# A Mamba-2 block with a LoRA branch on one core: the group norm's root and reciprocal on four rows, spread through DRAM, and the convolution one step later

## The chip, the core and the metric

The kernel runs on one core of a Trainium2 chip, in fp32 throughout. The metric is the device time of one execution in microseconds (us). The core has a matrix engine (PE in the profile, with its weight loads shown apart as PEld), a vector engine (DVE), a scalar engine (ACT), a general engine (POOL) and SyncE (SP), which here only issues DMAs. Each engine takes its own instructions in a fixed order, and semaphores hold an instruction until what it needs is there.

## What is computed

For 2048 tokens of width 1024, with `xn = layernorm(x)`:

```python
proj = xn @ in_proj_w.T                    # gate 4096 | x 4096, B 1024, C 1024 | dt 64
xBC  = silu(depthwise_conv4(proj[4096:10240]) + bias)
state_t = state_{t-1} * exp(dt*A) + (dt*x_t) B_t        # 64 heads of 64, 8 groups
y_t  = C_t . state_t + D * x_t
var  = mean(y_g * y_g) over the 512 channels of each of 8 groups
yn   = y_g * rsqrt(var + 1e-5) * norm_weight * silu(gate)
out  = x + yn @ out_proj_w.T + (xn @ W_base.T + b_base + top-2 of 8 LoRA experts of rank 16)
```

The change touches the line `yn = ...`: how the root and the reciprocal are made, one number for each token and group.

## The kernel before

The channels lie on the 128 partitions and the tokens along the free dimension. All big products are done by a seven-product Strassen-Winograd scheme; one product of the scheme is eight `MATMUL` records (four steps of the contraction, each two records in fp32).

The work falls into three stretches. A start (to about 180 us) normalizes the first 1024 tokens and makes the first products. The long middle (to about 2685 us) does two things at once: a *stream* of in-projection products (`stream`, `pair`, lines 450 to 495), and the scan. The last stretch is the out-projection.

The scan goes over 32 *blocks*: two halves of the sequence s, eight groups g, two halves of 512 tokens. A block has four *slots* c = 0 to 3 of 128 tokens. The loop at lines 983 to 1078 writes the order of a slot by hand: one product of the stream; `scan_b` of this slot (the products `ps_y`, `ps_e`, `ps_st` and the additions on DVE after them); the first third of `scan_a` of the next slot (the decay scan L688); a second product; the second third (`ps_cb`, the copies L698, L700, L705 on ACT, the product L709 on DVE); two more products; the last third (the transposes `ps_xt`, the scalings `xdt` L720 and `xdd` L728 on ACT); and one more product in some slots. Side work is dealt out among these products in a list `parts`, one entry for each. The PE instructions, the Silu activations and the scalings L720 and L728 keep this program order. For the others it is only a priority: the framework's planner orders each engine's instructions before the run, and may put one ahead of its place if it expects it to be ready. Nothing is reordered while the kernel runs.

A product's result waits in one of four PSUM buffers until DVE or ACT takes it. The seventh product of a scheme adds into the buffer that the fifth one left: DVE must have added that one out (`ev`, L531) within the one product that lies between.

The side work that matters here, for block b:

- Slot 0: `norm_mean` of the block before (L810): one matmul with a matrix of ones sums 512 channels of squares onto all 128 partitions (`ps_nv`), and ACT takes the root to `rms` (128x512, L815). Then `norm_gate` (L818), one step to each of the products 1, 2 and 3 and the last ones after them: the reciprocal on 128x512 (L821), four multiplications by the norm's weight and `rms` (L824), two by the gate (L832), each followed by the store of two channel tiles to DRAM (`y<-xg`, L833).
- Slots 1 and 2: `conv` of the next block (L629), seven steps, called four and four times (the eighth finds nothing left). A step is three DVE operations (L646) on one channel tile; steps 1 and 2 are for B and C (`bc`), steps 3 to 6 for x (`xg`). Step 3 also issues the first tap of all four x tiles on ACT (L640). The tile `xg` has two buffers, so the next block's convolution writes where the block before had its y: it waits until both stores `y<-xg` have landed.
- Slot 3: the squares of this block (L804, L806, L807).
- Blocks 2, 5, 8 and 11 load a piece of the second 1024 tokens into the gate's buffer (`sg`) in slot 1 and normalize it. Blocks 3, 6, 9 and 12, in slot 0, turn that piece's small projection into dt and decays: a chain of some 25 short DVE operations (L311 to L329, the polynomial L323 among them), whose exponential `ex` (L330) ACT must make.

Besides the four buffers of the stream, PSUM has four banks with one buffer each, called `y`, `e`, `st` and `aux`. Before the change `aux` serves `ps_cb`, `ps_xt` and `ps_nv`; `st` serves `ps_st`, the layer norm's sums, `ps_tot` and `ps_sm`.

Of the kernel before, what the change touches and what calls it, by code (L numbers as in the profile page):

```python
# [8 lines left out]
F32 = mybir.dt.float32  # L9
AF = mybir.ActivationFunctionType  # L10
# [5 lines left out]
H = 64  # L16
# [11 lines left out]
P = 128  # L28
TS = 1024
NS = L // TS  # L30
TB = 512
Q = 128
NQ = TB // Q
# [5 lines left out]
NSM = H + NE + NE * RANK  # L39
# [3 lines left out]
def mamba_lora_kernel(  # L43
# [17 lines left out]
    nc = tc.nc  # L61
# [16 lines left out]
    def mm(*args, **kw):  # L78
        tc.keep_in_program_order(nc.tensor.matmul(*args, **kw))  # L79
# [11 lines left out]
    ones = const.tile([P, P], F32, name="ones")  # L91
    nc.vector.memset(ones, 1.0)
    ident = const.tile([P, P], F32, name="ident")
    make_identity(nc, ident)
    eps = const.tile([P, 1], F32, name="eps")
    nc.vector.memset(eps, EPS)


# [87 lines left out]
    def over_channels(of, bank, name):  # L186
        ps = ps_one.tile([P, 2 * Q], F32, tag=bank, name=f"ps_{name}")
        for k, part in enumerate(of):
            mm(ps, ones, part, start=(k == 0), stop=(k == len(of) - 1))
        return ps  # L190
# [53 lines left out]
    def ln_next(s, i):  # L244

        t = piece_of[s, i]
        flat = t.rearrange("p k n q -> p k (n q)")

        of = halved(flat, f"{s}_{i}", ev, "ev")
        yield  # L250
        ps = over_channels(of, "st", f"mean_{s}_{i}")
        mean = lp.tile([P, 2 * Q], F32, tag="lnmean", name=f"mean_{s}_{i}")
        nc.scalar.activation(mean, ps, AF.Copy, scale=1.0 / DM)
        yield
        sqs = []
        for h in range(2):
            normal(flat[:, 4 * h : 4 * h + 4, :], mean, ALU.subtract)
            for k in (4 * h, 4 * h + 2):
                sq = ev.tile([P, 2, 2 * Q], F32, tag="ev", name=f"lsq_{s}_{i}_{k}")
                nc.scalar.activation(sq, flat[:, k : k + 2, :], AF.Square)  # L260
                sqs.append(sq)
            nc.vector.tensor_tensor(sqs[2 * h], sqs[2 * h], sqs[2 * h + 1], ALU.add)
            if h:
                nc.vector.tensor_tensor(sqs[0], sqs[0], sqs[2], ALU.add)
            yield
        ps = over_channels([sqs[0][:, 0, :], sqs[0][:, 1, :]], "st", f"var_{s}_{i}")
        std = lp.tile([P, 2 * Q], F32, tag="lnstd", name=f"std_{s}_{i}")
        nc.scalar.activation(std, ps, AF.Sqrt, bias=eps, scale=1.0 / DM)
        nc.vector.reciprocal(std, std)
        yield  # L270
        for h in range(2):
            normal(flat[:, 4 * h : 4 * h + 4, :], std, ALU.mult)
            yield
        b11, b12 = t[:, 0:KH, 0, :], t[:, 0:KH, 1, :]
        b21, b22 = t[:, KH:KT, 0, :], t[:, KH:KT, 1, :]
        cols = slice(i * Q, (i + 1) * Q)
        t4, t1, t2, t3 = (
            ev.tile([P, KH, Q], F32, tag="ev", name=f"t_{s}_{i}_{j}") for j in range(4)
        )
        nc.vector.tensor_tensor(t1, b12, b11, ALU.subtract)  # L280
        nc.vector.tensor_tensor(t2, b22, t1, ALU.subtract)
        yield
        nc.vector.tensor_tensor(t4, b21, t2, ALU.subtract)
        nc.vector.tensor_tensor(t3, b22, b12, ALU.subtract)
        for j, src in enumerate((b11, b21, b22, t4, t1, t2, t3)):
            nc.sync.dma_start(xop_d[s][j][:, :, cols], src)
        yield
# [9 lines left out]
    def small(s, i, chunks, sm, home):  # L297
# [32 lines left out]
        nc.scalar.activation(ex, at, AF.Exp)  # L330
        yield

        ps = ps_one.tile([P, nch, H], F32, tag="st", name=f"ps_tot_{n}")
        mm(
            ps.rearrange("p c h -> p (c h)"), ones, at.rearrange("p c h -> p (c h)"),
            start=True, stop=True,
# [268 lines left out]
    def steps(gen, n):  # L605

        return [lambda: next(gen, None) for _ in range(n)]
# [71 lines left out]
    def scan_a(s, g, half, c):  # L679

        key = s, g, half, c
        n = f"{s}_{g}_{half}_{c}"
        dab, ecp = decay_of.pop(key)
        hs = slice(g * HG, (g + 1) * HG)
        cs = slice(c * Q, (c + 1) * Q)

        es = p1.tile([P, HG, Q], F32, tag="es", name=f"es_{n}")
        nc.vector.tensor_tensor_scan(  # L688
            es.rearrange("p h t -> p (h t)"), dab.rearrange("p h t -> p (h t)"), here, 0.0,
            ALU.mult, ALU.add,  # L690
        )
        yield
        xg, bc = xbc_of[s, g, half]
        psm = ps_one.tile([P, 2, Q], F32, tag="aux", name=f"ps_cb_{n}")
        mm(psm[:, 0, :], bc[:, 0, cs], bc[:, 1, cs], start=True, stop=True)
        transpose(psm[:, 1, :], bc[:, 0, cs])
        cbm = p2.tile([P, Q], F32, tag="cbm", name=f"cbm_{n}")
        nc.scalar.copy(cbm, psm[:, 0, :])  # L698
        bt = p2.tile([P, Q], F32, tag="bt", name=f"bt_{n}")
        nc.scalar.copy(bt, psm[:, 1, :])  # L700

        psy = ps_one.tile([P, 4, Q], F32, tag="y", name=f"ps_y_{n}")
        for j in range(4):
            at = 4 * g + j
            nc.scalar.activation(  # L705
                psy[:, j, :], xg[:, j, cs], AF.Copy, scale=dsk[:, at : at + 1]
            )
        ms = dab
        nc.vector.tensor_tensor(  # L709
            ms, es, cbm.unsqueeze(1).to_broadcast([P, HG, Q]), ALU.mult  # L710
        )
        yield
        pst = ps_one.tile([P, 4, Q], F32, tag="aux", name=f"ps_xt_{n}")
        for j in range(4):
            transpose(pst[:, j, :], xg[:, j, cs])
        xdt = p2.tile([P, HG, HP], F32, tag="xdt", name=f"xdt_{n}")
        x_t = pst.rearrange("p j (a q) -> p (j a) q", q=HP)
        for h in range(HG):
            at = g * HG + h
            ins = nc.scalar.activation(  # L720
                xdt[:, h, :], x_t[:, h, :], AF.Copy,
                scale=dt_of[s][:, half * NQ + c, at : at + 1],
            )
            tc.keep_in_program_order(ins)

        xdd = p1.tile([P, HG, HP], F32, tag="xdd", name=f"xdd_{n}")
        for h in range(HG):
            ins = nc.scalar.activation(  # L728
                xdd[:, h, :], xdt[:, h, :], AF.Copy, scale=es[:, h, Q - 1 : Q]
            )  # L730
            tc.keep_in_program_order(ins)
        mid_of[key] = ms, ecp, bt, xdt, xdd, psy
        yield
# [74 lines left out]
        yield  # L808

    def norm_mean(s, g, half):  # L810
        y = y_of[s, g, half]
        ps = ps_one.tile([P, TB], F32, tag="aux", name=f"ps_nv_{s}_{g}_{half}")
        mm(ps, ones, y[:, 0, :], start=True, stop=True)
        std = p1.tile([P, TB], F32, tag="rms", name=f"rms_{s}_{g}_{half}")
        nc.scalar.activation(std, ps, AF.Sqrt, bias=eps, scale=1.0 / (4 * P))  # L815
        norm_of[s, g, half] = std

    def norm_gate(s, g, half):  # L818

        xg, std = xbc_of[s, g, half][0], norm_of[s, g, half]  # L820
        nc.vector.reciprocal(std, std)  # L821
        yield
        for j in range(4):
            nc.vector.scalar_tensor_tensor(  # L824
                xg[:, j, :], xg[:, j, :], nw[:, 4 * g + j : 4 * g + j + 1], std,
                ALU.mult, ALU.mult,
            )
        yield
        at = s * TS + half * TB
        for j in (0, 2):  # L830
            two = xg[:, j : j + 2, :]
            nc.vector.tensor_tensor(two, two, sg_of[s, g, half][:, j : j + 2, :], ALU.mult)  # L832
            nc.sync.dma_start(y_d[g][:, j : j + 2, at : at + TB], two)  # L833
            yield
# [148 lines left out]
    for b, blk in enumerate(blocks):  # L983
# [16 lines left out]
        for c in range(NQ):  # L1000
# [16 lines left out]
            if c in (1, 2) and nxt:  # L1017
                if c == 1:
                    conv_steps = conv(*nxt)
                side += steps(conv_steps, 4)  # L1020
            if c == 2 and after != 0:
                side += [lambda: load_gate(*blk)]
            if b == 1 and c < 2:
# [17 lines left out]
                load_decays(*second)  # L1041
            next(a, None)
            if c == 0 and prev:
                out = norm_gate(*prev)
                parts[1:4] = [[*p, lambda: next(out, None)] for p in parts[1:4]]
                parts[3] += [lambda: next(out, None)] * 2
            if c == NQ - 1:
                sq = norm_squares(*blk)
                parts[1] += steps(sq, 2)
# [18 lines left out]
                next(ln)  # L1068
            if after == 0 and c == 3:
                sm = lp.tile([P, 2, NSM], F32, tag="sm", name=f"sm_{piece[0]}_{piece[1]}")  # L1070
                ps = ps_one.tile([P, 2, NSM], F32, tag="st", name=f"ps_sm_{piece[1]}")
                for h in range(2):
                    small_mm(ps[:, h, :], lambda k: piece_of[piece][:, k, h, :])
                nc.scalar.copy(sm, ps)
                rest = small(*piece, slice(piece[1], 2 * NQ, NQ), sm, home)
                load_gate(*blk)
            if (after, c) in ((1, 1), (2, 0)):
                next(rest)
    norm_mean(*blocks[-1])
    for _ in norm_gate(*blocks[-1]):  # L1080
        pass
    wo_ctx.close()
# [325 lines left out]
```

## Time and profile before

| | |
|---|---|
| median of 3 runs | 3439.4 us (3437.9 to 3439.51) |
| the profiled execution | 3437.5 us, of which span 3435.7 us (1.8 us around it) |
| PE busy | 3404.6 us, 99% of the span |
| DVE busy | 2410.5 us, 70% |
| ACT busy | 1338.9 us, 39% |
| POOL busy | 697.2 us, 20% |
| reciprocal of the norm, L821 | 32 of 3345 ns |
| root of the norm, L815 | 32 of 687 ns |
| sum of the norm, `ps_nv` | 64 records (two for each block), 33.0 us busy |
| clock granted to PE | 0.998 of full speed |

The profile is one execution. Busy time is the time in which an engine has at least one instruction under way; for PE the ends of the matmuls are modelled, so an interval between two starts is often the better measure. A wait is idle time of an engine just ahead of an instruction, put down to whatever released it last. A number in square brackets in a timeline row is such a wait.

### The profile page before, as it was taken

How to read it: one execution, taken by the hardware profiler on the slowest of the kernel's cores; microseconds unless marked ns; L12 is line 12 of the kernel's file. 1: busy time of each engine (PE TensorE's matmuls, PEld its weight loads, DVE VectorE, ACT ScalarE, POOL GpSimd, SP SyncE). 2: the span in 40 equal slices, each digit the busy share in tenths (PEclk: the TensorE clock that was granted, in tenths of full speed). 3: DMA queues.
4: the chain of work that ended last, by engine and by line, in shares of the span. 5: the costliest groups of instructions: out<-in, count | busy, mean ns of one | idle time of the engine just before them, and what ended most of it. 6: DMA issues, size and time to landing. Idle time of an engine off the chain costs nothing.

```text
span 3435.7 us, 38674 instructions
## 1 busy us (share of the span) xinstructions
PE 3404.6 (99%) x12820; PEld 1989.8 (58%) x12820; DVE 2410.5 (70%) x2733; ACT 1338.9 (39%) x3694; POOL 697.2 (20%) x443
## 2 busy tenths in 40 slices
PE   9999999999999999999999999999999999999999
PEld 7444544544545544544455454454454588888888
DVE  7547776877877867777777877777875466566665
ACT  2245454554555454545545455555453000000000
POOL 4123223222222211332222332222321000000000
PEclk9999999999999999999999999999999999999999
DMA  6546655655666676887778787877777777585654
GB/s 236 190 166 198 209 184 187 216 183 196 207 196 209 196 261 219 287 261 242 235 246 256 235 255 249 254 237 240 242 237 260 256 274 242 195 300 187 214 164 144
DMA packets 530327, 769.85 MB, mean 224 GB/s; under 512 B 35152, under 2 KB 264656, under 8 KB 527440
## 3 DMA queue, kind: packets, MB, share of 16 engines
q1 hardware_dynamic: 530128, 767.39, 68.7%
q8 instruction: 102, 1.67, 0.2%
q14 instruction: 97, 0.79, 0.1%
HBM read 516.64 MB, written 250.61 MB: 223 GB/s over the span
## 4 chain that ended last, share of the span: by engine, by line
PE 87%; DVE 8%; issue 2%; DMA 2%; ACT 2%; SPq 0%; DVEq 0%; ACTq 0%
PE ps_x_x L79 12%; PE ps_x_w L79 8%; PE ps_a_x L79 8%; PE ps_y_x L79 8%; PE ps_x_g L79 8%; PE ps_y_w L79 6%; PE ps_a_w L79 6%; PE ps_y_g L79 5%; PE ps_a_g L79 5%; PE ps_y L79 3%; PE ps_e L79 3%; PE ps_st L79 3%; PE ps_x_b L79 2%; DVE xg L646 2%; PE ps_a_b L79 2%
## 5 line engine op out<-in xcount | busy, mean ns | idle before, releaser
L83 POOL TENSOR_TENSOR state<-state,tot 128x512 f32<-128x512 f32 x112 | 150.2, 1341 | 1307.6 <-PE ps_e L79 1175.7
L688 DVE TENSOR_TENSOR_SCAN es<-dab,here 128x1024 f32<-128x1024 f32 x128 | 303.5, 2371 | 82.6 <-ACT xdd L728 81.3
L646 DVE SCALAR_TENSOR_TENSOR xg<-rawx,cw,xg 128x512 f32<-128x512 f32 x384 | 338.3, 929 | 16.8 <-ACT xg L640 15.9
L79 PE MATMUL ps_x_w<-t,w 128*128 128x256 f32 x1344 | 303.8, 379 | 0.0
L720 ACT ACTIVATE xdt<-ps_xt,dt 128x64 f32<-128x64 f32 x1024 | 223.0, 331 | 203.6 <-PE ps_xt L88 203.6
L79 PEld LDWEIGHTS ps_x_w<-t,w 128*128 128x128 f32 x1344 | 255.4, 190 | 41.5 <-issue 7.7
L705 ACT ACTIVATE ps_y<-xg,dsk 128x128 f32<-128x128 f32 x512 | 190.2, 371 | 222.5 <-DVE xg L770 192.9
L1345 ACT COPY s<-ps_a_w 128x512 f32<-128x512 f32 x28 | 16.4, 585 | 636.2 <-PE ps_a_w L79 555.6
L728 ACT ACTIVATE xdd<-xdt,es 128x64 f32<-128x64 f32 x1024 | 261.7, 387 | 0.0
L83 POOL TENSOR_TENSOR wo<-wo 128x512 f32<-128x512 f32 (+1 forms) x112 | 211.9, 1892 | 6.8
L709 DVE TENSOR_TENSOR dab<-es,cbm 128x1024 f32<-128x1024 f32 x128 | 177.6, 1388 | 39.3 <-ACT cbm L698 39.0
L79 PE MATMUL ps_a_w<-q,w 128*128 128x256 f32 x896 | 202.5, 379 | 0.0
L79 PEld LDWEIGHTS ps_a_w<-q,w 128*128 128x128 f32 x896 | 170.2, 190 | 23.6 <-issue 0.5
L79 PE MATMUL ps_x_x<-op_again,s_x 128*128 128x512 f32 x384 | 172.7, 592 | 0.0
L79 PE MATMUL ps_y_x<-op_again,s_x 128*128 128x512 f32 x384 | 172.7, 592 | 0.0
L79 PE MATMUL ps_a_x<-op_again,a_x 128*128 128x512 f32 x384 | 172.7, 592 | 0.0
L79 PEld LDWEIGHTS ps_y<-dab,xdt 128*64 128x64 f32 x2048 | 112.8, 137 | 102.9 <-issue 40.8
L79 PE MATMUL ps_x_x<-op,s_x 128*128 128x512 f32 x368 | 165.5, 592 | 0.0
L79 PE MATMUL ps_y_x<-op,s_x 128*128 128x512 f32 x368 | 165.5, 592 | 0.0
L79 PE MATMUL ps_a_x<-op,a_x 128*128 128x512 f32 x368 | 165.4, 592 | 0.0
L646 DVE SCALAR_TENSOR_TENSOR bc<-rawb,cw,bc 128x512 f32<-128x512 f32 x192 | 163.8, 885 | 1.9 <-ACT bc L640 1.3
L531 DVE TENSOR_TENSOR ev<-ps_x_x,s_x 128x512 f32<-128x512 f32 x94 | 64.4, 686 | 129.3 <-PE ps_x_x L79 124.2
(238 smaller groups left out, 6152.1 us busy)
## 6 DMA issues: line engine op xcount, KB each, us to landing
w<-w SPq DMA_DIRECT2D x196, 512.0 KB, 3.7
dab<-da_d SPq DMA_DIRECT2D x128, 512.0 KB, 5.4
raw<-ev SPq DMA_DIRECT2D x192, 256.0 KB, 3.3
a_x<-in_w_in_dram SPq DMA_DIRECT2D x168, 256.0 KB, 4.0
w<-wo SPq DMA_DIRECT2D x96, 448.0 KB, 4.3
ecp<-run_d SPq DMA_DIRECT2D x256, 128.0 KB, 4.0
gate<-ev SPq DMA_DIRECT2D x128, 256.0 KB, 3.6
sg<-gate SPq DMA_DIRECT2D x32, 1024.0 KB, 7.8
```

Source lines behind the costliest of these rows:

```text
L79: tc.keep_in_program_order(nc.tensor.matmul(*args, **kw))
L83: ins = nc.gpsimd.tensor_tensor(*args)
L531: nc.vector.tensor_tensor(e, ps, add, alu)
L646: nc.vector.scalar_tensor_tensor(dst[:, i, :], raw[:, i, k : k + TB], cw[:, ti, k : k + 1], dst[:, i, :], ALU.mult, ALU.add,)
L688: nc.vector.tensor_tensor_scan(es.rearrange("p h t -> p (h t)"), dab.rearrange("p h t -> p (h t)"), here, 0.0, ALU.mult, ALU.add,)
L705: nc.scalar.activation(psy[:, j, :], xg[:, j, cs], AF.Copy, scale=dsk[:, at : at + 1])
L709: nc.vector.tensor_tensor(ms, es, cbm.unsqueeze(1).to_broadcast([P, HG, Q]), ALU.mult)
L720: ins = nc.scalar.activation(xdt[:, h, :], x_t[:, h, :], AF.Copy, scale=dt_of[s][:, half * NQ + c, at : at + 1],)
L728: ins = nc.scalar.activation(xdd[:, h, :], xdt[:, h, :], AF.Copy, scale=es[:, h, Q - 1 : Q])
L1345: nc.scalar.copy(s1, pa)
```

## The change

The norm's sum is made with four matmuls instead of one. Matmul c has as its weights four columns of which only column c is ones, and 128 tokens as its moving operand; together they leave a tile of 4 rows of 128 tokens. Root and reciprocal are made on this 4x128 tile. A new function `norm_spread` makes the reciprocal, stores the tile to DRAM (2 KB) and loads it back to all 128 partitions (256 KB written). It is called in slot 0; `norm_gate` moves to slot 1, all three steps ahead of the convolution's there. The convolution makes three steps in slot 1 and four in slot 2. The transposes `ps_xt` move to the bank `st`; the layer norm's sums, `ps_tot` and `ps_sm` move from `st` to `aux`.

```diff
-    eps = const.tile([P, 1], F32, name="eps")
+    row_of = const.tile([P, 8], F32, name="row_of")
+    nc.vector.memset(row_of, 0.0)
+    nc.vector.memset(row_of[:, NQ - 1 : NQ], 1.0)
+    eps = row_of[:, 7:8]
     nc.vector.memset(eps, EPS)
...
-        ps = over_channels(of, "st", f"mean_{s}_{i}")
+        ps = over_channels(of, "aux", f"mean_{s}_{i}")
...
-        ps = over_channels([sqs[0][:, 0, :], sqs[0][:, 1, :]], "st", f"var_{s}_{i}")
+        ps = over_channels([sqs[0][:, 0, :], sqs[0][:, 1, :]], "aux", f"var_{s}_{i}")
...
-        ps = ps_one.tile([P, nch, H], F32, tag="st", name=f"ps_tot_{n}")
+        ps = ps_one.tile([P, nch, H], F32, tag="aux", name=f"ps_tot_{n}")
...
-        pst = ps_one.tile([P, 4, Q], F32, tag="aux", name=f"ps_xt_{n}")
+        pst = ps_one.tile([P, 4, Q], F32, tag="st", name=f"ps_xt_{n}")
...
     def norm_mean(s, g, half):
         y = y_of[s, g, half]
-        ps = ps_one.tile([P, TB], F32, tag="aux", name=f"ps_nv_{s}_{g}_{half}")
-        mm(ps, ones, y[:, 0, :], start=True, stop=True)
-        std = p1.tile([P, TB], F32, tag="rms", name=f"rms_{s}_{g}_{half}")
-        nc.scalar.activation(std, ps, AF.Sqrt, bias=eps, scale=1.0 / (4 * P))
-        norm_of[s, g, half] = std
+        n = f"{s}_{g}_{half}"
+        ps = ps_one.tile([NQ, Q], F32, tag="aux", name=f"ps_nv_{n}")
+        for c in range(NQ):
+            mm(
+                ps, row_of[:, NQ - 1 - c : 2 * NQ - 1 - c], y[:, 0, c * Q : (c + 1) * Q],
+                start=(c == 0), stop=(c == NQ - 1),
+            )
+        rms = p1.tile([P, TB], F32, tag="rms", name=f"rms_{n}")
+        nc.scalar.activation(
+            rms[0:NQ, 0:Q], ps, AF.Sqrt, bias=eps[0:NQ], scale=1.0 / (4 * P)
+        )
+        norm_of[s, g, half] = rms
+
+    def norm_spread(s, g, half):
+        rms = norm_of[s, g, half]
+        std = rms[0:NQ, 0:Q]
+        n = f"{s}_{g}_{half}"
+        nc.vector.reciprocal(std, std)
+        std_d = dram.tile([NQ, Q], F32, tag=f"std_d_{n}", name=f"std_d_{n}")
+        nc.sync.dma_start(std_d, std)
+        nc.sync.dma_start(
+            rms, std_d.rearrange("c t -> (c t)").unsqueeze(0).to_broadcast([P, TB])
+        )
...
-        xg, std = xbc_of[s, g, half][0], norm_of[s, g, half]
-        nc.vector.reciprocal(std, std)
-        yield
+        xg, rms = xbc_of[s, g, half][0], norm_of[s, g, half]
         for j in range(4):
             nc.vector.scalar_tensor_tensor(
-                xg[:, j, :], xg[:, j, :], nw[:, 4 * g + j : 4 * g + j + 1], std,
+                xg[:, j, :], xg[:, j, :], nw[:, 4 * g + j : 4 * g + j + 1], rms,
                 ALU.mult, ALU.mult,
             )
...
-                side += steps(conv_steps, 4)
+                side += steps(conv_steps, 3 if c == 1 else 4)
...
             if c == 0 and prev:
+                parts[1].insert(0, lambda: norm_spread(*prev))
+            if c == 1 and prev:
                 out = norm_gate(*prev)
-                parts[1:4] = [[*p, lambda: next(out, None)] for p in parts[1:4]]
-                parts[3] += [lambda: next(out, None)] * 2
+                parts[1][:0] = steps(out, 3)
...
-                ps = ps_one.tile([P, 2, NSM], F32, tag="st", name=f"ps_sm_{piece[1]}")
+                ps = ps_one.tile([P, 2, NSM], F32, tag="aux", name=f"ps_sm_{piece[1]}")
...
     norm_mean(*blocks[-1])
+    norm_spread(*blocks[-1])
     for _ in norm_gate(*blocks[-1]):
         pass
```

## The prediction, made before the changed kernel was built or run

> **What bounds the kernel now.** I read the engines' busy time first, for the engine at its limit.
>
> ```profile
> PE 3404.6 (99%) x12820; PEld 1989.8 (58%) x12820; DVE 2410.5 (70%) x2733; ACT 1338.9 (39%) x3694; POOL 697.2 (20%) x443
> ```
>
> PE is busy in all but 31 us of the span. A change that unloads DVE and ACT can gain only what PE now waits for them. So the second view is PE's waits between 180 and 2690 us, the scan (in all, times, longest):
>
> ```profile
> PE ps_y L79 <- ACT xdt L720: 6.9, 5, 4.6
> PE ps_x_x L79 <- DVE ev L531: 3.6, 3, 1.3
> PE ps_x_g L79 <- DVE ev L531: 3.3, 6, 1.1
> PE ps_e L79 <- ACT da L346: 1.7, 2, 0.9
> PE ps_st L79 <- ACT xdd L728: 1.4, 4, 0.4
> PE ps_mean L79 <- DVE half L183: 1.0, 1, 1.0
> PE ps_nv L79 <- ACT xdt L720: 0.6, 1, 0.6
> ```
>
> Some 19 us, and no DMA among them. Third, the timeline at the longest of these waits (block 3, end of slot 0), from the answers for DVE, ACT and PE:
>
> ```profile
> 431.08 3.35 DVE L821 RECIPROCAL rms<-rms 128x512 f32<-128x512 f32 x1
> ...
> 442.44 1.21 DVE L832 TENSOR_TENSOR xg<-xg,sg 128x1024 f32<-128x1024 f32 x1
> ...
> 448.30 0.28 DVE L329 TENSOR_TENSOR at<-dt,na 128x128 f32<-128x128 f32 x1
> ...
> 449.02 0.31 ACT L330 ACTIVATE ex<-at 128x128 f32<-128x128 f32 x1
> 449.24 1.73 ACT L720 ACTIVATE xdt<-ps_xt,dt 128x64 f32<-128x64 f32 x8
> ...
> 449.59 0.69 PE L79 MATMUL ps_y<-dab,xdt 128*64 128x128 f32 x3 [4.57 <-ACT xdt L720]
> ```
>
> The releaser is ACT, but ACT was idle: it stood at the exponential L330, which waited for the polynomial on DVE, and DVE had the reciprocal and the norm's multiplications in the same slot (busy 24.70 of the 26 us from 424 on). The later waits for `xdt` at the end of slot 0 (blocks 6, 9 and 12: 0.7, 0.4 and 0.7 us) have the same order of rows. The waits for `ev` lie elsewhere: five of nine in slot 1 of the later half. Fourth, block 24 by slots (from a slot's first `ps_y` to the next):
>
> ```profile
> 2084.60:2105.50 20.90, 20.90 (x74) 10.36 (x73) 17.73 (x17) 8.61 (x27) 1.04 (x1) 1.00 0.68 216
> 2105.50:2124.50 19.00, 17.77 (x68) 8.90 (x67) 15.89 (x19) 10.93 (x29) 7.18 (x5) 1.00 0.68 206
> 2124.50:2142.00 17.50, 17.50 (x68) 8.87 (x67) 7.64 (x8) 6.64 (x24) 5.70 (x3) 1.00 0.88 299
> 2142.00:2161.40 19.40, 18.64 (x70) 9.07 (x69) 15.59 (x16) 10.68 (x30) 5.65 (x3) 1.00 0.76 221
> ```
>
> The fourth figure after the window is DVE's busy time: 17.7, 15.9, 7.6, 15.6 us. Slot 2 stands half empty. The chain there runs reciprocal, norm multiplications, `y<-xg` (2099.19, 5.03 us), the next block's convolution until 2119, `ev` at 2120.12, and PE waits 1.23 us.
>
> **Part by part.** The rows for the prices:
>
> ```profile
> L821 DVE RECIPROCAL rms<-rms 128x512 f32<-128x512 f32 x32 | 107.0, 3345 | 0.9 <-ACT rms L815 0.9
> L318 DVE RECIPROCAL u<-u 128x128 f32<-128x128 f32 x4 | 3.8, 952 | 0.0
> L79 PE MATMUL ps_e<-bc,state 128*128 128x128 f32 x960 | 139.9, 289 | 1.7 <-ACT da L346 1.7
> L79 PE MATMUL ps_nv<-sq,ones 128*128 128x512 f32 x64 | 33.0, 597 | 0.7 <-ACT xdt L720 0.6
> ```
>
> *Reciprocal.* Three quarters of the elements in a row go: 3.345 - 0.952 = 2.39 us a block, 77 us of DVE in all, none of it on PE's path except at the waits above. The root falls from 0.687 us to about that of the 128x128 exponential (0.31): 12 us of ACT, beside PE's work.
>
> *The moved multiplications.* Four of 0.74 and two of 1.2 us, 5.4 us a block, leave their place in slot 0. With the reciprocal that is 7.8 us less DVE before the polynomial's end in blocks 3, 6, 9 and 12. The exponential was late by 4.6 us at most. Gain: 4.6+0.7+0.4+0.7 = 6.4, the `ps_st` waits that follow three of them, 3 x 0.36 = 1.1, and the slow records after the longest. On that last: the Trainium skill ("TensorE: Matmul & The Clock Gate", What's actually happening) says that the clock halves after an idle window of about 3.4 us; after the 4.6 us wait the starts of the next six or so records lie 1.2 us further apart than elsewhere, and after none of the waits under 2 us. Sum 8.7 us. What is late next there: `ev`, 2.6 us before the exponential, not waited for. Bounds: 0, if the planner moves the multiplications back ahead of the polynomial and they wait for the load, to 8.7. I take 8: DVE has 7.8 us of room for a delay of 4.6.
>
> *Banks.* `ps_nv` no longer waits for `xdt` (0.6), nor the first `ps_xt` for the copy `bt` (0.6): gain 1.2. `ps_xt` now waits for the state's addition L784, which in block 24 ends at 2091.9, 6 us ahead of it: 0. The moved sums wait for the copies of L700, done a product earlier: 0. Without that cover each would cost a copy, 0.3 us.
>
> *Sum on PE.* Two records of 512 columns become eight of 128. Here a rule speaks against the change. The same page (Back-to-back issue gap) gives for sustained matmuls 81 ns at 128 columns and 131 at 512, so quartering a matmul makes it 4 x 81/131 = 2.5 times as long: from the trace's two starts (429 and 522 ns, 0.95 us) to 2.35 us, +1.4 a block, +45 us in all. The trace says otherwise: starts lie 429 ns apart at 512 columns and 112 (median) to 128 (mean) at 128 columns in `ps_e`, whose weights also change with each matmul. By that, eight take 0.90 to 1.02 us: -2 to +2 us in all. The row decides; I take 0. The extreme bound is a weight load of 190 ns unhidden at each, 1.52 us, +18 in all; `ps_e` excludes it.
>
> *Spread.* Two more DMAs a block, 64 in all, on SP. A small store (`s_x_d<-s_x`) lands in 2.1 us, `run_d` in 4.1; loads of the broadcast kind in 4.0 (`ecp`) to 5.4 us (`dab`). So `rms` is there 6 to 9.5 us after the reciprocal, I take 7.5. The skill's "DMA: Bandwidth & Descriptors" (Anatomy of one DMA) has 2.0 us fixed and 436 GB/s, an estimate of 4.6 us for both: by that the multiplications could start in block 24 at 2093.7, as they do now (2093.56); by the rows at 2096 to 2098. SP stands still for the reciprocal and the store's landing, 2 to 4 us a block, and behind it lie weights (L423), stores of results (L535) and decays (L665, L673). It stands still as long already (up to 9.6 us for POOL, 7.0 for DVE), and PE waits for no DMA in the scan, since weights are loaded a pair ahead: 0. Without that cover it would be 31 x 3 = 93 us.
>
> *Norm and convolution later.* From DVE's free time in slot 0 the planner may take the multiplications as soon as it expects `rms`, so y lands 3 us later than now at the least, or a slot (18) at the most. Half of the convolution's 11 us on `xg` falls into slot 2, where DVE is idle 9.9 of 17.5 us. Silu of `xg` ends at 2131.4 in block 24, its readers begin at 2147.8: 16 us of cover, 0. The gate buffer is free later for the pieces, which land at 359.4 and 616.5, 15 us before their first use (375.1, 631.0): 0. Unhidden, they would cost up to 3 us in each of four blocks.
>
> *`ev` waits in slot 1* (1.09, 1.31, 1.23, 0.68, 1.10: 5.4 us): less convolution in the slot, but possibly the multiplications. Bounds: all gone, -5.4; or 1.2 us in each of the 31 slots, +37. I take 0, nearest to the rows: as much work leaves as may come.
>
> *End.* The last block's multiplications move from 2682.6 to about 2687, and the loads behind them. PE has base products until 2726; the first operand made from those loads is ready at 2697.7 now: 0.
>
> Sum: 3437.5 - 8 - 1.2 = 3428.3 for the profiled execution, which stands 1.9 us below the median; against the median 3439.4 - 9.2 = 3430.
>
> **Rivals.**
>
> *A, gain and more:* the shorter chain also ends the slot-1 waits: 9.2 + 5.4, 3425. For it: slot 2 is empty and the convolution moves there. Against: the chain is longer by the DMAs.
>
> *B, gain given back in slot 1:* the multiplications run there, 5.4 in against at most 2.8 us out. DVE fills that slot already in the later half, so about 1 us more of `ev` in nine blocks eats the gain: 3439. Against: slot 0 has room for them.
>
> *C, slower:* DVE comes to the multiplications before `rms` has landed and stands still, with `ev` queued behind. PE gives `ev` one product, 3.4 us, less its 0.7: beyond 2.7 us of standing still PE waits for the rest. At the slow ends (9.5 against the 4.6 hoped for) that is 4.9 - 2.7 = 2.2 us, in those blocks where one of two products in seven stands there: 31 x 2/7 x 2.2 = 20, and the gain at the exponential is lost as well, as the polynomial stands behind too: 3439 + 20 - 1 = 3458. For it: ACT already stands up to 5.0 us for `y<-xg` at L640, so the planner is too hopeful of landings. Against: slot 0 has DVE time to catch up.
>
> **Numbers.** The likeliest 3430, 0.36 (own range 3426 to 3432); A 0.12; B 0.25; C 0.27. Two tenths of a percent, 6.9 us, is about what a measurement can tell from no change. Faster by more takes the first two, 0.48; B is within it, 0.25; C is slower, 0.27. The range reaches from A's upper part, 3423, into C, 3453.
>
> **What would show it.** Right: `RECIPROCAL` at about 0.95 us; PE's wait for `xdt` under 1 us in all; eight `ps_nv` records starting within 0.9 to 1.02 us; DVE's waits for `rms` under 1 us each; `ev` waits of about 7 us in all. Wrong: DVE waits of 3 us and more for `rms<-std_d`, `ev` waits over 15 us, or any PE wait for a weight's DMA.

## The result: 20 us slower, and the profile after

The changed kernel takes 3458.9 us (median of six runs, 3456.8 to 3461.9) against 3438.8 us of the kernel before (six runs beside it, 3437.5 to 3439.5): ratio 1.006, 95% interval 1.0047 to 1.0073. Forecast were 3430 and a range that ended at 3453. The profiled execution takes 3461.9 us, its span 3460.1 us, 24.4 more than the one before. From here on, line numbers of the changed kernel stand four or more higher than in the kernel before: L825 is the root, L835 the reciprocal, L837 and L838 the two DMAs of the spread, L846 the norm's multiplications, L854 the product with the gate, L855 the store of y, L644 and L650 the convolution on ACT and DVE, L187 the last half sum of the layer norm.

Busy time first, from the page of the changed kernel.

```profile
PE 3414.7 (99%) x13012; PEld 2002.3 (58%) x13012; DVE 2342.5 (68%) x2735; ACT 1326.5 (38%) x3693; POOL 705.3 (20%) x443
```

DVE has lost 68 us of work, as wanted, and the kernel is slower all the same. The waits say where; these are PE's between 180 and 2710 us of the changed kernel (us in all, times, longest).

```profile
PE ps_y L79 <- ACT xdt L724: 9.0, 6, 3.3
PE ps_mean L79 <- ACT xdd L732: 6.4, 3, 2.8
PE ps_x_g L79 <- DVE ev L535: 5.4, 6, 1.3
PE ps_x_x L79 <- DVE ev L535: 4.4, 2, 2.5
PE ps_st L79 <- ACT xdd L732: 2.9, 7, 0.8
PE ps_var L79 <- ACT xdt L724: 2.8, 1, 2.8
PE ps_mean L79 <- DVE half L187: 2.4, 1, 2.4
```

They sum to 33.3 us against 18.5. What is new is the group `ps_mean` and `ps_var`, the layer norm's sums in blocks 2, 5, 8 and 11: 11.6 us, where there was 1.0. "ACT xdd" as the releaser is only the event that came last: in block 2 the half sum on DVE ends at 381.57 us and `ps_mean` starts at 381.72, so DVE's `half` is what it needed. The same stretch of the changed kernel, DVE's waits:

```profile
DVE xg L846 <- DMA rms<-std_d: 45.0, 24, 6.1
DVE xg L650 <- ACT xg L644: 23.2, 17, 2.8
```

and one of ACT's:

```profile
ACT xg L644 <- DMA y<-xg: 66.3, 23, 6.8
```

Before, the last two were 4.5 us in 3 and 20.6 us in 10, and the first did not exist. So the convolution's first tap on ACT stands for the stores of y, and DVE's taps stand behind it. The pieces that were to get cheaper did so, as these groups of the changed kernel show:

```profile
L79 PE MATMUL ps_nv<-sq,row_of 128*4 128x128 f32 x256 | 33.2, 273 | 0.0
L835 DVE RECIPROCAL rms<-rms 4x128 f32<-4x128 f32 x32 | 29.7, 928 | 3.9 <-ACT rms L825 3.9
L825 ACT ACTIVATE rms<-ps_nv,row_of 4x128 f32<-4x128 f32 x32 | 11.4, 358 | 25.3 <-PE ps_nv L79 25.0
```

And block 24 by slots, the same cut as before (the fourth figure after the window is DVE's busy time):

```profile
2106.90:2127.90 21.00, 21.00 (x77) 10.41 (x75) 15.02 (x16) 7.32 (x26) 1.04 (x1) 1.00 0.68 216
2127.90:2147.50 19.60, 17.71 (x68) 8.84 (x67) 15.85 (x19) 10.99 (x29) 7.18 (x5) 1.00 0.71 227
2147.50:2165.00 17.50, 17.50 (x68) 8.87 (x67) 7.36 (x8) 7.58 (x25) 5.69 (x3) 1.00 0.87 289
```

Slot 0 is 2.7 us emptier, slots 1 and 2 are as they were: the planner kept the multiplications in slot 0 (116 of the 124 that were written into slot 1 start there) and the convolution in slot 1.

PE keeps its program order, so the blocks of two kernels can be compared one by one. The table has PE's waits of over 0.5 us, before and after, and by how much the blocks are longer (+) or shorter (-) than before, counted from a block's first `ps_y` to the next block's, in the changed kernel and in four kernels of the experiments below (one execution each, us). The lengths also count what the waits leave out.

| blocks | waits before, after | the change | e2 | e10 | e13 | e18 |
|---|---|---|---|---|---|---|
| 3, 6, 9, 12 | 7.8, 3.3 | -9.8 | -8.3 | -11.8 | -9.2 | -11.8 |
| 2, 5, 8, 11 | 1.0, 12.7 | +18.9 | +4.8 | +17.5 | +6.2 | +7.0 |
| the others up to 14 | 0, 3.1 | +4.1 | +0.8 | +3.1 | +3.3 | +2.7 |
| 15 to 30 | 6.8, 11.7 | +12.2 | +4.8 | +5.2 | +8.7 | +3.1 |

The first line is the gain that was forecast, and it came. The other three are the loss: over half of it in four blocks, a third in the later half.

**Where most of it is made: block 2.** Five rows of the kernel before, from the timelines of SP, ACT, DVE and PE.

```profile
351.53 1.50 SPq L833 DMA_DIRECT2D y<-xg  x2
354.07 1.58 SPq L114 DMA_DIRECT2D piece<-in_xT_dram  x2
...
356.90 2.95 ACT L640 ACTIVATE xg<-rawx,cb,cw 128x512 f32<-128x512 f32 x4
...
376.44 0.69 DVE L183 TENSOR_TENSOR half<-half,half 128x512 f32<-128x512 f32 x1
...
377.55 1.03 PE L79 MATMUL ps_mean<-half,ones 128*128 128x256 f32 x4
```

Both stores of y leave together, then the loads of the next piece; the first tap of the convolution follows, and the half sums, behind it on DVE, are done at 377.13, 0.42 us before PE takes them. The same stretch of the changed kernel, from DVE, SP, ACT, DVE and PE:

```profile
353.33 2.35 DVE L854 TENSOR_TENSOR xg<-xg,sg 128x1024 f32<-128x1024 f32 x2
...
354.58 0.37 SPq L855 DMA_DIRECT2D y<-xg  x1
355.71 0.38 SPq L118 DMA_DIRECT2D piece<-in_xT_dram  x1
...
358.81 0.33 SPq L539 DMA_DIRECT2D raw<-ev  x1
...
360.21 0.72 SPq L855 DMA_DIRECT2D y<-xg  x1
...
366.44 0.81 ACT L644 ACTIVATE xg<-rawx,cb,cw 128x512 f32<-128x512 f32 x1 [4.34 <-DMA y<-xg]
...
380.89 0.68 DVE L187 TENSOR_TENSOR half<-half,half 128x512 f32<-128x512 f32 x1
...
381.72 1.31 PE L79 MATMUL ps_mean<-half,ones 128*128 128x256 f32 x4 [2.76 <-ACT xdd L732]
```

The last product with the gate ends at 355.68, but its store leaves SP only at 360.21: it stands in SP's queue behind the piece's loads and behind a result's store (`raw<-ev`, 358.81) that waits for its operand. The order is that of the loop: `load_piece` is called at the head of slot 1, and `norm_gate`, moved from slot 0 into slot 1, now comes after it. The first tap starts 9.5 us later than before, the convolution's last step ends 7.5 later, the half sums 4.4, and PE's sum starts 4.2 later; 1.2 us of each is the later start of the block.

### The profile page after: what moved, and what is told of

Its sections match the earlier page's. It is cut to its first block, busy times and chain, and to the rows that moved or that the text cites. A ratio compares the mean times of both kernels' runs of the same rounds, so it can differ in the third digit from the quotient of the medians.

```text
span 3460.1 us, 39333 instructions
## 1 busy us (share of the span) xinstructions
PE 3414.7 (99%) x13012; PEld 2002.3 (58%) x13012; DVE 2342.5 (68%) x2735; ACT 1326.5 (38%) x3693; POOL 705.3 (20%) x443
## 4 chain that ended last, share of the span: by engine, by line
PE 82%; DVE 6%; DMA 4%; issue 4%; ACT 2%; POOL 1%; SPq 1%; DVEq 0%; POOLq 0%; ACTq 0%
PE ps_x_x L79 11%; PE ps_x_w L79 8%; PE ps_y_x L79 8%; PE ps_a_x L79 8%; PE ps_x_g L79 7%; PE ps_y_w L79 6%; PE ps_a_w L79 6%; PE ps_y_g L79 4%; PE ps_a_g L79 4%; PE ps_y L79 3%; PE ps_e L79 3%; PE ps_st L79 2%; PE ps_x_b L79 2%; DVE xg L650 2%; PE ps_a_b L79 2%
## 5 line engine op out<-in xcount | busy, mean ns | idle before, releaser
L650 DVE SCALAR_TENSOR_TENSOR xg<-rawx,cw,xg 128x512 f32<-128x512 f32 x384 | 327.9, 905 | 34.0 <-ACT xg L644 33.4
L650 DVE SCALAR_TENSOR_TENSOR bc<-rawb,cw,bc 128x512 f32<-128x512 f32 x192 | 166.3, 901 | 4.6 <-ACT bc L644 4.2
L79 PE MATMUL ps_y<-dab,xdt 128*64 128x128 f32 x2048 | 147.5, 284 | 9.0 <-ACT xdt L724 9.0
```

Of the source, the lines that this page charges most:

```text
L650: nc.vector.scalar_tensor_tensor(dst[:, i, :], raw[:, i, k : k + TB], cw[:, ti, k : k + 1], dst[:, i, :], ALU.mult, ALU.add,)
```

## The experiments

All of them were timed beside the kernel before (its median was 3438.8 to 3439.8 us in each group of runs). "Trip" is the way of the reciprocal through DRAM; "place" is the multiplications a slot later together with the convolution a step later.

**e1, the banks alone** (the five lines with `"aux"` and `"st"` of the diff, nothing else).

> The kernel before with the five bank moves alone. Theory T (the trip through DRAM makes the norm's multiplications, the stores of y and the next convolution late): no change, 3436 to 3442 us. Theory P (the multiplications and the convolution stand a slot later in the program): the same. Theory B (the banks: the layer norm's sums and the transposes now wait for other readers): most of the 20 us, 3452 or more, with PE waits at ps_mean and ps_var.

Measured: 3438.3 us, ratio 0.9999 (0.9991 to 1.0008). None of the 20 us lies in the banks.

**e2, four rows and trip, in the old place and the old banks.**

```diff
+                parts[1].append(lambda: norm_spread(*prev))
+                parts[2].append(lambda: next(out, None))
+                parts[3] += [lambda: next(out, None)] * 3
```

> Four rows and the trip through DRAM, but the multiplications in slot 0 where they were, four convolution steps in slot 1, and the old banks. T: as slow as the changed kernel or slower, 3455 to 3470, DVE waiting 50 us or more for rms<-std_d. P: the loss goes with the place, 3430 to 3440. B: 3430 to 3440.

Measured: 3440.7 us, 1.0007 (0.9998 to 1.0015). No difference, although DVE waits 53.0 us for the spread here too. But the table above shows that this is a balance: blocks 3, 6, 9 and 12 are 8.3 us shorter, the others 10.4 longer.

**e3, the place alone,** with the 128x512 reciprocal and no trip.

```diff
+                parts[1].insert(0, lambda: next(out, None))
+            if c == 1 and prev:
+                parts[1][:0] = steps(out, 3)
...
+                side += steps(conv_steps, 3 if c == 1 else 4)
```

> No trip: root and reciprocal on 128x512 as before, but the multiplications in slot 1 and three convolution steps there, old banks. T: no loss, 3432 to 3442. P: most of the loss, 3450 to 3460, with PE waiting for ev in slot 1.

Measured: 3446.9 us, 1.0025 (1.0015 to 1.0035). The place alone costs 8 us. PE's waits for `ps_mean` are 5.0 us.

**e4 and e9, meant to take DVE's wait for the spread away,** at the late place (e4, made from the change) and at the old one (e9, made from e2).

```diff
-                xg[:, j, :], xg[:, j, :], nw[:, 4 * g + j : 4 * g + j + 1], rms,
+                xg[:, j, :], xg[:, j, :], nw[:, 4 * g + j : 4 * g + j + 1], here[:, 0:TB],
```

> The changed kernel, both DMAs of the spread issued, but the multiplications read a constant tile in place of rms, so that the norm's factor is left out of the result and nothing waits for the load. T: most of the loss is gone, 3430 to 3442; DVE's wait for rms (51 us) and most of ACT's wait for y<-xg (66 us) vanish. P and B: 3452 to 3460 still.

> e2 (four rows and the trip, everything else in its old place) with the multiplications reading a constant tile, so that the norm's factor is left out of the result: what the shorter root and reciprocal are worth when the trip is not waited for. Theory G (the prediction's gain at the end of slot 0 is real, and the wait for rms eats it): 3429 to 3434 us. Theory N (there is nothing to gain, or re-planning gives it back elsewhere): 3437 to 3442, as e2.

Measured: 3446.7 us, 1.0023 (1.0014 to 1.0033), and 3453.7 us, 1.0039 (1.0026 to 1.0053). Neither answers its question. With nothing to wait for, the planner moved the multiplications into slot 3 of the block before and the convolution up with them, so the order changed with the wait. That multiplications free to run early came out 13 us *slower* in e9 than in e2 is a warning: earlier is not better by itself.

**e5, the old place in blocks 2, 5, 8 and 11 only,** the change elsewhere (both lists of e2 and of the change, chosen by `after == 0`).

> The changed kernel, but in the four blocks that normalize a piece of the second half (2, 5, 8, 11) the multiplications and the convolution steps stand where they stood before. Theory L (most of the loss is in these four blocks, where the piece's sums queue behind the late convolution in slot 1): 3442 to 3447 us, 14 us less than the changed kernel, with PE waits at ps_mean and ps_var of about 1 us. Theory E (the loss is spread evenly over all 31 blocks): 31/35 of it stays, 3455 to 3458.

Measured: 3451.1 us, 1.0036 (1.0024 to 1.0048): 8 us less than the change, where theory L had 14. At the start of block 15 this kernel is 13.4 us ahead of the changed one, but from there to block 31 it loses 15.0 us to the kernel before, the changed one 12.2: the later half came out differently though the edit does not touch it.

**e6 and e7, the product with the gate written to the gate's buffer,** so that the stores of y hold `sg` and not `xg`: from the change (e6) and from the kernel before (e7).

```diff
-            two = xg[:, j : j + 2, :]
-            nc.vector.tensor_tensor(two, two, sg_of[s, g, half][:, j : j + 2, :], ALU.mult)
+            two = sg_of[s, g, half][:, j : j + 2, :]
+            nc.vector.tensor_tensor(two, xg[:, j : j + 2, :], two, ALU.mult)
```

> The changed kernel, but the last product of the norm is written to the gate's tile and stored from there, so that the convolution waits for DVE's product and not for the store's landing. Theory Y (what costs is that the stores y<-xg land late and the convolution, with ACT's and DVE's later work, stands behind them): ACT's wait of 66 us at L644 falls under 20, 3440 to 3447. Theory H (what costs is DVE standing for rms at the head of its queue): 3454 to 3460.

> The kernel before with the same edit. Y: ACT's 21 us at L640 vanish and with them most of the 6.8 us of PE waits in slot 1 of the later blocks, 3431 to 3436. H: nothing to gain, 3437 to 3441.

Measured: 3456.5 us, 1.0051 (1.0038 to 1.0063), and 3450.1 us, 1.0031 (1.0019 to 1.0042). In e6 ACT's waits for `y<-xg` are gone, with 40.3 us for DVE's product with the gate in their place. PE's waits of over 0.5 us in blocks 2, 5, 8 and 11 fall from 12.7 to 3.4 us, as they should if the stores are their cause, but those for `xdt` rise from 9.0 to 13.8. In e7, where nothing was late, the first tap in those blocks starts some 5 us earlier; in blocks 3, 6, 9 and 12 the convolution's steps on `xg` now come in among the polynomial's, and there PE waits 14.7 us for `xdt`, up to 6.3 at once. A release that comes earlier again made the kernel slower.

**e8, e11 and e12, an earlier spread:** sum, root and spread in slot 3 of the own block, in the old banks (e8) and in the new (e11); and the spread straight behind the sum in slot 0, one product earlier (e12). All three have the old place.

```diff
+            if c == NQ - 1:
+                parts[3] += [lambda: norm_mean(*blk), lambda: norm_spread(*blk)]
```

> Four rows and the trip, but sum, root, reciprocal and trip at the end of slot 3 of the same block, and the multiplications in slot 0 where they stood before, old banks. If the exposed trip is what ate the gain from the shorter reciprocal (e2 was even with the kernel before): DVE's wait for rms under 5 us in all, 3428 to 3434. If the shorter reciprocal gives nothing: 3437 to 3442.

> e8 with the changed kernel's banks, so that the transposes after the sum no longer share its bank. If e8's loss was that bank alone: PE's 45 us of waits at ps_xt go, and with the trip hidden 3430 to 3438. If the early sum itself is the trouble (it stands before the last squares are done): still 3450 or more.

> e2 with reciprocal and trip written straight after the sum, one product earlier. If the trip's exposure is what matters: DVE's wait for rms falls from 53 us to under 30, 3433 to 3438. If the planner had already put them there: no change, 3438 to 3442.

Measured: 3530.1 us, 1.0265 (1.0251 to 1.0279); 3485.6 us, 1.0135 (1.0122 to 1.0149); 3447.2 us, 1.0023 (1.0014 to 1.0031). The first of PE's waits in e8 names what the move of banks is for:

```profile
PE ps_xt L88 <- ACT rms L825: 45.0, 31, 3.6
```

In one bank the transposes wait for the root, in every block. In e11 that wait is gone and 45 us with it, yet 46 remain, with DVE still standing 51.9 us for the spread; which of the other waits (`xdt` 14.3, `ps_mean` 9.1) comes from what stays open. In e12 DVE waits 61.3 us for the spread, 8 more than in e2; a likely reason, not shown, is that what is started earlier is also expected earlier.

**e10, the change with the convolution's steps as before.**

```diff
-                side += steps(conv_steps, 3 if c == 1 else 4)
+                side += steps(conv_steps, 4)
```

> The changed kernel with four convolution steps in slot 1 again. If the later step is part of the loss (it leaves the convolution of the block behind other work): 3448 to 3454. If it is a help, because it keeps work out of slot 1: 3464 or more. If it is nothing: 3456 to 3461.

Measured: 3453.0 us, 1.0046 (1.0034 to 1.0059), 6 us less than the change. The gain is not in the four blocks (PE's waits for `ps_mean` and `ps_var` are 12.8 us): the waits over 0.5 us from block 15 on fall from 11.7 to 7.4 us, and the one of block 3 from 3.3 to 1.6. By their lengths, blocks 15 to 30 are 7.0 us shorter than in the change.

**e13, the change with the stores of y first** in the planner's order whenever they are ready.

```diff
+            with tc.high_priority():
+                nc.sync.dma_start(y_d[g][:, j : j + 2, at : at + TB], two)
```

> The change as it is, but the two stores of y of a block are given first place among what is ready, so that they stand as early as possible in SP's order. Theory (the loss in blocks 2, 5, 8 and 11 is the second store's place on SP, behind loads of pieces and results that wait): those blocks lose about 10 us less, 3447 to 3451. Rival (the trip through DRAM itself makes the convolution and the half sums late there): 3456 to 3460, with the same waits of PE for the half sums. Second rival (any other order is as likely worse): 3455 to 3465, with new waits elsewhere.

Measured: 3448.3 us, 1.0022 (1.0015 to 1.0029), 10.6 us less than the change and within the theory's figures. Of the 14.8 us between the spans of the two profiled executions, 12.7 lie in blocks 2, 5, 8 and 11, as the theory had it. Block 2 of this kernel, from the timelines of SP, ACT, DVE and PE:

```profile
355.76 1.51 SPq L856 DMA_DIRECT2D y<-xg  x2
...
360.15 2.93 ACT L644 ACTIVATE xg<-rawx,cb,cw 128x512 f32<-128x512 f32 x4 [0.86 <-DMA y<-xg]
...
378.69 0.69 DVE L187 TENSOR_TENSOR half<-half,half 128x512 f32<-128x512 f32 x1
...
379.80 1.03 PE L79 MATMUL ps_mean<-half,ones 128*128 128x256 f32 x4
```

With DVE and the trip as late as in the change, both stores leave together, ACT waits 0.86 us in place of 4.34, and PE not at all.

**e14 and e15, without the trip:** e2 and the change, with a write of the whole tile on DVE in place of the two DMAs.

```diff
-        nc.sync.dma_start(std_d, std)
-        nc.sync.dma_start(
-            rms, std_d.rearrange("c t -> (c t)").unsqueeze(0).to_broadcast([P, TB])
-        )
+        nc.vector.memset(rms, 1.0)
```

> Leaves out the way through DRAM: the root and the reciprocal of the four rows are made, and then the whole tile is set to 1.0 on DVE, so the multiplications use a factor of 1. The multiplications and the convolution stand where they stand in the kernel before. What the shorter reciprocal alone is worth, had it no trip. Theory (the trip ate a gain of about 8 us that was there): 3430 to 3434. Rival (the shorter reciprocal is worth nothing, since PE hardly waits for DVE): 3437 to 3441.

> Leaves out the way through DRAM in the same manner (the tile is set to 1.0 on DVE), with multiplications and convolution a slot later, as in the change. Theory (late place costs 8 us, the trip 12 on top of it): 3445 to 3449. Rival (the loss is all in the place, the trip nothing): 3456 to 3460. Second rival (the trip is all of it): 3435 to 3440.

Measured: 3438.1 us, 0.9996 (0.9987 to 1.0004), and 3443.7 us, 1.0011 (1.0003 to 1.0019). In e14 the theory fell and its rival held: in the whole kernel the shorter reciprocal is worth at most 4.5 us even with no trip at all, so the trip had no gain of 8 to eat. In block 3 of e14 DVE loses 1.1 us more to a wait for `bc` (1.46 us after 0.36), 0.5 to the write, and 1.8 to two operations that take 1.55 and 1.75 us where others of their kind take 0.74; that is more than the 2.4 us of the reciprocal, and PE waits 5.5 us for `xdt`, 4.6 before. In e15 the time lies just under the theory's figures: the late place without the trip costs 4 us. Against the 20.1 of the change and the 1.5 of e2, the trip costs 16 us at the late place and 3 at the old.

**e16, e2 with the spread's DMAs and the stores of y first,** meant to beat both kernels.

> The four-row root and reciprocal with the trip, multiplications and convolution where they stand before, and the trip's two DMAs and the stores of y given first place among what is ready. If SP's order is what eats the gain of the shorter reciprocal at the old place: 3431 to 3436. If the trip's own length (about 6 us) eats it: 3439 to 3442.

Measured: 3446.9 us, 1.002 (1.0013 to 1.0026). Both expectations missed: it is 6 us slower than e2. First place is no gift where nothing was late (PE waits 3.1 us for `ps_mean`); why it is as much as 6 us was not settled.

**e17 and e18, the stores of y first** in e3 (place alone), and in e10 (the change with the convolution's old steps).

> Only the place of the change (multiplications a slot later, convolution one step later), with the full 128x512 reciprocal and no trip, as in e3, and the stores of y given first place among what is ready. Theory (e3's 8 us come through the second store's place on SP): 3438 to 3442. Rival (the place costs by itself, the convolution being later whatever the stores do): 3445 to 3448, as e3.

> The change with the convolution's steps as before (e10, 6 us less) and the stores of y first (e13, 11 us less). If the two losses are apart they add up: 3441 to 3444. If both are one loss, the late convolution, seen from two sides: 3447 to 3450, as e13 alone.

Measured: 3443.4 us, 1.0014 (1.0008 to 1.0021), and 3441.0 us, 1.0005 (0.9997 to 1.0013). In e17 the store is somewhat under half of the place's 8 us, between both expectations: PE's waits for `ps_mean` fall from 5.0 to 1.0 us, but blocks 15 to 30 stay 5.6 us longer than before, 5.1 in e3. The convolution's later step may be the rest, but it was not undone there. e18 says that the two losses of the change add up: with both mended, the difference from the kernel before is within its interval.

## Why the prediction was wrong

In blocks 2, 5, 8 and 11 (means over the four, us from the start of slot 0, from the traces; PE's waits are those of all four):

| kernel | time | gate product ends | second store issued | first tap on ACT | conv of x ends | PE waits, `ps_mean` and `ps_var` |
|---|---|---|---|---|---|---|
| before | 3438.8 | 14.0 | 14.0 | 19.1 | 35.1 | 1.0 |
| e2 (trip) | 3440.7 | 17.1 | 17.1 | 20.7 | 36.3 | 2.6 |
| e3 (place) | 3446.9 | 14.0 | 20.1 | 25.2 | 39.2 | 5.0 |
| e17 (place, stores first) | 3443.4 | 14.0 | 14.0 | 18.7 | 35.7 | 1.0 |
| the change | 3458.9 | 17.1 | 22.9 | 28.7 | 44.0 | 11.6 |
| e13 (stores first) | 3448.3 | 17.1 | 17.2 | 20.5 | 36.7 | 2.7 |

The trip makes the products 3 us later and the place makes the second store leave 6 us after them. Either alone is taken up in part (PE waits 2.6 and 5.0 us for the sums), both together are not (11.6): that is why 2 and 8 do not sum to 20. The 20 us are, by what gave them back: the second store's place in SP's queue, 11 (e13); the convolution's later step, some 6 to 7 (e10, and e18 against e13); what is left, 2, no larger than its interval. They are a balance: against the gain of 9.8 us in blocks 3, 6, 9 and 12 stand 35 us of longer blocks elsewhere.

*Norm and convolution later, "0": the step that failed.* Its cover was wrongly chosen. It looked at the readers of the convolution (16 us) and at the landing of the pieces (15 us), which both held. It did not look at what else DVE has queued behind the convolution, the half sums, ready only 0.4 us before PE used them in block 2 and late by 1.0 us in block 5: the row `ps_mean <- half`, 1.0, stood in the table that was quoted. And "y lands 3 us later at the least, or a slot at the most" spoke of DVE only: the store too was moved, past the piece's loads on SP. Put at nothing, the move cost 18.9 us in the length of blocks 2, 5, 8 and 11, with PE waiting 11.6 us for the half sums, and the larger part of the 12.2 us of the later half, of which e10 gave back 7.0.

*SP stands still, "0": half wrong.* PE indeed waits for no DMA of weights. But SP's queue also holds the stores of y, and its delays reach PE by way of ACT, DVE and `half`, where no row names a DMA.

*Gain at the end of slot 0, 8 us: right in place and size, not in all of its way.* Blocks 3, 6, 9 and 12 are 9.8 us shorter. PE's waits there fall by 6.0 us (4.5 of them in waits over 0.5 us); of the 7.5 us that the step named, 3.3 remain. The 1.7 us of `ps_e <- da`, in blocks 6 and 12, are among those that went, a row that was quoted and left out of the sum. In block 3 of the changed kernel (DVE, ACT, PE):

```profile
453.36 0.27 DVE L333 TENSOR_TENSOR at<-dt,na 128x128 f32<-128x128 f32 x1
...
453.66 0.31 ACT L334 ACTIVATE ex<-at 128x128 f32<-128x128 f32 x1 [4.67 <-DVE at L333]
...
454.22 2.17 PE L79 MATMUL ps_y<-dab,xdt 128*64 128x128 f32 x16 [3.29 <-ACT xdt L724]
```

The wait is 3.3 us in place of 4.6. The chain is the predicted one, but the multiplications did not leave slot 0; they still run ahead of the polynomial's end, at 445.8 to 452.6 us, which the step had named as its lower bound, with a gain of 0. For the waits of 0.4 to 0.7 us in blocks 6, 9 and 12 the shorter reciprocal, 2.4 us, would do alone. So part of the agreement in size is luck; how the rest of the 9.8 us comes about stays open.

*Banks, 1.2: nothing* (e1). The waits named there are too small to see in the time.

*Sum on PE, 0 (bounds -2 and +2): right for the eight, somewhat over with what stands ahead of them.* Eight records take 0.97 us from the first start to the next matmul, where two took 0.95. But the first of them starts 523 ns after the matmul ahead, 429 before, so the sum is 0.11 us dearer in a block, some 3.4 us in all. The ratio of 81 to 131 ns in the Trainium skill ("TensorE: Matmul & The Clock Gate", Back-to-back issue gap) would have given 45; these records start as far apart as those of `ps_e`, as argued.

*Spread, 7.5 us after the reciprocal: right.* The first multiplication starts 7.3 us (median) after the reciprocal's end; store to load 3.1, load to landing 3.8. The estimate of 4.6 from the Trainium skill ("DMA: Bandwidth & Descriptors", Anatomy of one DMA) is too short; the section gives its figures for DMAs that the general engine issues, and these are issued by SP. DVE does stand for it, 2 us at a time and up to 6.1, as rival C said, against "under 1 us" of the forecast. But at the old place the whole trip costs about 3 us (e2 against e14), and of its 16 at the late place e13 gives back 11 with DVE standing no less (55.9 us).

*`ev` waits, 0: 2.9 us too low* (9.8 after 6.9), within the bounds.

*The rivals.* C, 3458, has the measured time by another mechanism. Its products in slot 0 that wait for `ev` behind `rms` are not where PE stands; the half sums are. Its argument that the planner is too hopeful of landings (ACT's 5.0 us for `y<-xg`) did point to the queue that decided: that wait became 66.3 us in all. B's point, that the gain is given back elsewhere, is what e2 shows (8.3 us shorter in four blocks, 10.4 longer in the others), though not in slot 1 alone.

What stays open is why the convolution's later step costs 6 to 7 us, most of it in the later half, where DVE's order differs in many places at once, and the 46 us of e11.

## What to carry to other kernels

When a step is moved in the program, list each queue that it enters, and look for what is now ahead of it there: a store moved past a load can cost more than the arithmetic. Cover has to be measured at everything queued behind the delayed instruction, and first at the consumer that already waits a little, however small its row. With one engine at 99%, work taken off another is worth only the waits for it, and an order that is nearly free of waits is upset by earlier results as well as by later ones (e7, e9, e12).

## What the runs showed of the hardware beyond that

Four rows of 128 numbers cost DVE's reciprocal 928 ns, nearly as much as 128 rows (953 ns), while 128 rows of 512 cost 3345: in these shapes the length of a row counts and the number of rows hardly.

PE's clock falls after shorter waits than the prediction had it. These are stretches of 4 us of the changed kernel; the last figure but two is the clock granted to PE, as a share of full speed.

```profile
382.00:386.00 4.00, 4.00 (x26) 3.09 (x24) 2.38 (x2) 0.38 (x1) 0.00 (x0) 0.57 0.18 66
664.00:668.00 4.00, 4.00 (x12) 1.73 (x11) 2.29 (x1) 3.97 (x9) 0.52 (x1) 1.00 0.18 66
894.00:898.00 4.00, 3.47 (x20) 2.67 (x20) 3.19 (x4) 0.81 (x3) 0.00 (x0) 0.57 0.72 179
1618.00:1622.00 4.00, 4.00 (x7) 1.70 (x6) 2.66 (x5) 1.56 (x4) 0.00 (x0) 0.57 0.88 284
```

They follow waits of 2.76, 2.77, 2.75 and 2.51 us, in blocks 2, 5, 8 and 17. In three of them the trace has the clock at 0.5 for 3.4 us, in the second not at all. In the whole scan of the changed kernel there are five such stretches of 3.4 us, each beginning within 1.3 us of the end of a wait of 2.4 to 3.3 us; in that of the kernel before there is one, of 6.8 us, which begins in the wait of 4.57 us. In e13 the clock falls 1.4 us after the end of a wait of 2.68 us. Blocks 2, 8 and 17 are 1.9 to 2.0 us longer than their added waits explain; block 11, with an added wait of 0.9 us and the clock at 1.0 throughout, only 0.3. So a wait of some 2.5 us may cost PE 1.7 us more (an estimate: half of 3.4), which is part of what the waits alone do not explain in the 24 us between the profiled executions.
